# The opening of the Mamba stage: another order of transposes, softplus sums, copies, convolution and norm

## The chip, the cores and the metric

The kernel runs on one core of one Trainium2 chip. The metric is device time in microseconds (us) of one execution; the time before is 3008.5, the median of three runs (3007.97 to 3010.53). The engines are TensorE (PE, with its weight loads PEld), VectorE (DVE), ScalarE (ACT), GpSimd (POOL) and SyncE (SP, which issues DMAs). Each takes its own instructions in order and waits for the others by semaphores.

## The reference, cut to what matters

Four layers act on x of shape (2, 128, 56, 56), each as `x = x + layer(group_norm(x))`. Layer 0 is an attention, layer 1 a 3x3 convolution, layer 2 a mixture of experts on patches. Layer 3, in which the change lies, runs two Mamba blocks over the rows of the image, one from left to right and one from right to left, and fuses their outputs:

```python
xz = x @ in_w.T
xi, z = jnp.split(xz, 2, axis=-1)
xc = silu(conv_b + sum(xp[:, k:k + L, :] * conv_w[:, k] for k in range(K)))   # K = 4
dt, Bm, Cm = jnp.split(xc @ xproj_w.T, [DT_RANK, DT_RANK + D_STATE], axis=-1)
dt = softplus(dt @ dt_w.T + dt_b)
def step(h, inp):
    dA = jnp.exp(dt_l[:, :, None] * A)
    h = dA * h + (dt_l * u_l)[:, :, None] * B_l[:, None, :]
    return (h, jnp.einsum('bds,bs->bd', h, C_l))
y = (ys + xc * Dp) * silu(z)
return y @ out_w.T
```

The group norm in front of the layer needs the mean and the variance of a whole image, after the experts' results have been added to it.

## The kernel before, in words

The image is cut into 14 blocks of 448 positions (7 for each of the two images). In `mamba_pair` each block has two halves, forward (f) and backward (b), and each half 16 units: 8 pairs of states by 2 halves of the inner channels. For a unit, ScalarE computes `dA` (`decay`, two activations into PSUM), GpSimd `dBu` (`push`, the product of dtu and B, six buffers), VectorE scans (`scan`, L1939), and the state is multiplied by C, on VectorE from a PSUM copy `c_ps` (L1950, ScalarE writes the copy at L1927), or on GpSimd for the units listed in POOLED (L1948). TensorE sums the products into the PSUM tile `y` (`collect`, L1961; its first call also writes the skip term, L1957).

The order on every engine is written out by hand, in two stretches with a manual schedule. The first is the opening: steps below zero of an `agenda`, in which the first block's forward half is prepared. Its stages are the convolution (`conv`, into the banks "mm" and "c", 16 weight passes for both halves of the channels), `low`, `step`, `log`, `softplus` (a sum of four terms in PSUM by matmuls with the identity, L1874, and a copy of dt by ScalarE, L1875), `weigh` (dtu = dt * xc on VectorE, and a small memset of row starts on GpSimd) and `send_steps`: eight DMAs for each half of the channels, four that spread dtu (issued on SP) and four that spread dt (issued on GpSimd's queue). The second stretch is the loop over units; it also works off later agenda steps, each stage a few units ahead of its use: one TensorE operation, and its ScalarE copy one step later.

Among the opening's steps stands `arrive`, a generator for the second image: GpSimd gathers the experts' rows (g, 14 indirect DMAs), VectorE adds each pair of rows (L1486), TensorE transposes them (`y_ps`, L1489, four small transposes a block, seven blocks), VectorE adds them to x (L1462) and takes statistics (L88). After the seventh block follows the norm of the image (`norm_stages`: aggregate, two matmuls with a group matrix, and small VectorE and ScalarE operations, L66 to L110, and L1616 and L1617). A tuple of counts says how many pieces of this generator are worked off at each opening step. `back_bank` gives its PSUM from the "dA" banks while `opening` is true.

The first block's backward half has its convolution (`b.conv`) at opening steps 17, its Silu at step 19 (with a table load before and after), so that on the engines these stand among the first scans. The norm is first used by ScalarE when block 7 is prepared, some 190 units later.

Of the kernel before, what the change touches and what calls it, by code (L numbers as in the profile page):

```python
# [8 lines left out]
F32 = mybir.dt.float32  # L9
# [8 lines left out]
P = 128  # L18
# [1586 lines left out]
def arrive(net, combine, b, gathered, bank, banks, pool, norms, lead=0):  # L1605
    nc = net.nc
    yield from combine(b, gathered, bank, lead)
    got = []
    for n, stage in enumerate(net.norm_stages(b, banks, "mm", got.append)):
        fetch = stage()  # L1610
        if fetch:
            fetch()
        yield
    mean, rstd = got[0]
    both_of = pool.tile([P, 2], F32, name=f"norm{b}")
    nc.vector.scalar_tensor_tensor(both_of[:, 0:1], mean, -1.0, rstd, ALU.mult, ALU.mult)  # L1616
    nc.vector.tensor_copy(both_of[:, 1:2], rstd)  # L1617
    norms[b] = (both_of[:, 1:2], both_of[:, 0:1])


def mamba_pair(net, out, wts, combine, keep, norms):
# [19 lines left out]
    with ExitStack() as ctx:  # L1641
# [14 lines left out]

        def wide_bank(name):
            return ps.tile([P, 1024], F32, name=name, tag="dA", bufs=2)

        opening = True  # L1660

        def back_bank(name):
            return wide_bank(name) if opening else mm(name)

        class Banks:
            def tile(self, shape, dtype, name, tag):
                return back_bank(name)[:, :512]

        ps_of_norms = Banks()


        place = {"tag": "mm"}

        def mm(name):
            return ps.tile([P, 512], F32, name=name, tag=place["tag"])
# [93 lines left out]
        class Half:  # L1769
# [3 lines left out]
                self.blk, self.w = blk, w  # L1773
                self.dA, self.dBu, self.hc, self.C = {}, {}, {}, {}

            def conv(self, m, as_=AF.Identity):
                w = self.w
                pm = mm("conv_ps")
                for n in range(K):

                    at = n if w.d == "f" else 2 * (K - 1) - n
                    nc.tensor.matmul(
                        rows(pm[:, :BLK]),
                        w.conv[:, m, n, :],
                        self.blk.xn[:, :, at : at + HW],
                        start=n == 0,
                        stop=n == K - 1,
                    )
                if m == 0:
                    self.xc = work.tile([P, 2, BLK], F32, name="xc", tag=f"xc{w.d}", bufs=1 if w.d == "f" else 2)  # L1790
                return lambda: nc.scalar.activation(self.xc[:, m, :], pm[:, :BLK], as_, bias=w.conv_b[:, m : m + 1])
# [85 lines left out]
            def weigh(self, m=None):  # L1877

                some = slice(0, 2) if m is None else slice(m, m + 1)
                self.dtu = self.u  # L1880
                engine = nc.gpsimd if m is None else nc.vector
                engine.tensor_mul(self.dtu[:, some], self.dt[:, some], self.xc[:, some])

                at = 0 if self.w.d == "f" else HW - 1
                starts = self.dt[:, some].rearrange("p m (r t) -> p (m r) t", t=HW)[:, :, at : at + 1]
                nc.gpsimd.memset(starts, 1e31)

            def send_steps(self, m=None):

                some = slice(0, 2) if m is None else slice(m, m + 1)  # L1890
                if not m:
                    self.dt2 = work.tile([P, 2, 2, BLK], F32, name="dt2", tag="dt2")
                    self.dtu2 = work.tile([P, 2, 2, BLK], F32, name="dtu2", tag="dtu2")
                for to, src, queue in ((self.dtu2, self.dtu, nc.sync), (self.dt2, self.dt, nc.sync if m is None else nc.gpsimd)):
                    for s in range(2):
                        for r in range(2):
                            queue.dma_start(to[s * H : (s + 1) * H, some, r, :], src[r * H : (r + 1) * H, some, :])
# [87 lines left out]
        for n, blk in enumerate(blocks):  # L1985
# [3 lines left out]
            if n == 0:  # L1989
# [14 lines left out]
                    book(at + 12 + m, lambda f=f, m=m: f.send_steps(m))  # L2004
                for i, (h, m) in enumerate(((f, 0), (f, 1), (b, 0), (b, 1))):
                    book((1, 4, 5, 13)[i], lambda h=h, m=m: h.gate(m))
                book(at + 17, lambda b=b: b.conv(0))
                book(at + 17, lambda b=b: b.conv(1), tag="c")
                book(at + 19, lambda b=b: silu(b, None))
                for m in range(2):  # L2010
                    book(2 + 3 * m, lambda b=b, m=m: b.step(m))
                    book(4 + 3 * m, lambda b=b, m=m: b.log(m))
# [62 lines left out]

        E = mybir.EngineType
        with tc.manual_schedule(engines={E.PE, E.Activation, E.DVE, E.Pool, E.SP}):
            second = arrive(net, combine, 1, gathered, back_bank, ps_of_norms, keep, norms, LEAD2)
            first = min(agenda)
            for step in range(first, 0):  # L2080
                run(step)
                for _ in range((LEAD2, 0, 0, 0, 0, 0, 1, 0, 1, 2, 1, 1, 1, 2, 1, 1, 1)[step - first] if step - first < 17 else 0):
                    next(second, None)
                fetch(step + 1)
            opening = False
        with tc.manual_schedule(engines={E.PE, E.Activation, E.DVE, E.Pool, E.SP}):
            for h, u in units[:6:2]:
                h.send_c(u // 2)
# [3 lines left out]
            for n, (h, u) in enumerate(units):  # L2092
# [13 lines left out]
                if done:  # L2106
                    done.pop().close()
                waiting.append((h, u))

                quota = 0 if u == 3 and n > 3 else 2 if u == 7 and n > 7 else 1  # L2110
                for _ in range(quota):
# [124 lines left out]
```

## Time and profile before

| | |
|---|---|
| median of three runs | 3008.5 us |
| the profiled execution | 3005.48 us |
| its span on the core | 3003.3 us |
| TensorE, VectorE, ScalarE, GpSimd busy | 2679.8, 2187.2, 1851.7, 1450.4 us |
| the scans, L1939 | 448, 2.008 us each |
| dBu, L1920 | 448, 2.094 us each |
| first forward convolution of the Mamba stage | 1651.34 us |
| first scan | 1689.70 us |
| scan of unit 16 (first of the backward half) | 1752.98 us |
| last instruction's chain begins | 2962.88 us |

Times in the profile are microseconds from the span's start. In a row of a timeline the first number is the start, the second the length, then engine, line, operation, output and inputs, the number of instructions merged, and in brackets how long the engine had been idle and what ended that. A releaser is inferred; where the named engine had long been done, it was another. A table by stage gives for each stretch the busy time of each engine, the granted TensorE clock (1.00 is full), the share of DMA engines busy and GB/s.

### The profile page before, as it was taken

The numbers are of one execution on the slowest core, as the hardware profiler recorded it, in microseconds if no ns is written. First come the engines' busy times: TensorE is split into PE (matmuls) and PEld (weight loads), VectorE is DVE, ScalarE is ACT, GpSimd is POOL, SyncE is SP. The second block draws the span as 40 slices with busy tenths as digits, with TensorE's granted clock in tenths as the row PEclk, the third lists the DMA queues.
The fourth block names the chain that finished last, engine by engine and source line by source line (L and its number), as shares of the span: only waits on it lengthen the run. The fifth ranks groups of instructions, "written<-read, shape, count | busy, mean of one in ns | idle before, by whom it ended". The sixth has DMA issues, their size and how long they took to land. (4 is left out here: it accounts for less than half of the span.)

```text
span 3003.3 us, 39370 instructions
## 1 busy us (share of the span) xinstructions
PE 2679.8 (89%) x14926; PEld 1271.0 (42%) x14926; DVE 2187.2 (73%) x1856; ACT 1851.7 (62%) x2942; POOL 1450.4 (48%) x801
## 2 busy tenths in 40 slices
PE   7999999999989799999999788888888888888874
PEld 3333333333325688878777333333333333233321
DVE  5978999999886400000120589999999999999996
ACT  5778787888761100000011588888888888988884
POOL 3000010001322100000110789999999999999995
PEclk9999999999999799999999789999899999999997
DMA  1000000000002587878885644465554465544460
GB/s 56 1 1 1 1 1 1 1 1 1 1 1 61 224 316 295 330 295 329 312 300 211 146 112 115 121 142 140 118 121 118 115 145 131 127 116 121 116 149 23
DMA packets 157966, 369.30 MB, mean 123 GB/s; under 512 B 25190, under 2 KB 115014, under 8 KB 154166
## 3 DMA queue, kind: packets, MB, share of 16 engines
q1 hardware_dynamic: 135778, 339.30, 37.5%
q0 software_dynamic: 5520, 15.62, 1.7%
q10 hardware_dynamic: 16452, 11.61, 1.2%
q8 instruction: 122, 2.00, 0.3%
q14 instruction: 94, 0.77, 0.1%
HBM read 297.89 MB, written 17.20 MB: 105 GB/s over the span
## 5 line engine op out<-in xcount | busy, mean ns | idle before, releaser
L1920 POOL TENSOR_TENSOR dBu<-dtu,Bs 128x896 f32<-128x896 f32 x448 | 921.8, 2094 | 13.2 <-DVE h L1939 8.3
L1939 DVE TENSOR_TENSOR_SCAN h<-dA,dBu 128x896 f32<-128x896 f32 x448 | 881.7, 2008 | 25.9 <-ACT dA L1909 19.1
L620 ACT ACTIVATE ex<-sc 128x896 f32<-128x896 f32 (+1 forms) x700 | 602.6, 918 | 124.7 <-PE sc L617 113.4
L1961 PE MATMUL y<-h,both 128*64 128x448 f32 x1792 | 466.0, 611 | 81.8 <-POOL h L1948 74.3
L627 DVE TENSOR_TENSOR ex_sum<-ex_sum,ex 128x1792 f32<-128x1792 f32 (+1 forms) x238 | 492.6, 2070 | 35.2 <-ACT ex L620 21.2
L1380 PEld LDWEIGHTS h_ps<-xs_c,w 128*128 128x128 f32 x3584 | 406.6, 193 | 27.2 <-ACT ot L1403 16.2
L1380 PE MATMUL h_ps<-xs_c,w 128*128 128x128 f32 x3584 | 411.6, 277 | 6.9 <-DMA w<-in_L_conv_w_dram 5.3
L617 PE MATMUL sc<-q,k 32*128 32x448 f32 (+1 forms) x2800 | 403.6, 587 | 3.6 <-ACT ex L620 2.9
L1950 DVE TENSOR_TENSOR h<-h,c_ps 128x1792 f32<-128x1792 f32 (+1 forms) x168 | 326.6, 1944 | 26.7 <-ACT c_ps L1927 9.2
L635 PE MATMUL av<-ex,va 128*32 128x448 f32 (+1 forms) x2800 | 334.3, 552 | 0.1
L1394 DVE TENSOR_TENSOR ht<-h_ps,sg 128x512 f32<-128x512 f32 x56 | 38.5, 691 | 398.1 <-PE h_ps L1380 324.0
L582 POOL TENSOR_TENSOR a_e<-a_e,a_inv 112x784 f32<-112x784 f32 x14 | 41.6, 2973 | 583.3 <-ACT ex L620 394.5
L1909 ACT ACTIVATE dA<-dt,f_A 128x448 f32<-128x448 f32 x448 | 282.7, 636 | 58.4 <-DVE h L1939 45.5
L1909 ACT ACTIVATE dA<-dt,b_A 128x448 f32<-128x448 f32 x448 | 282.8, 635 | 34.9 <-DVE h L1939 25.5
L1961 PEld LDWEIGHTS y<-h,both 128*64 128x64 f32 x1792 | 118.3, 147 | 354.8 <-issue 209.0
L1314 POOL DMA_INDIRECT xr<-xd,whom x28 | 28.0, 1000 | 484.4 <-PE xr_ps L1369 444.5
L1948 POOL TENSOR_TENSOR h<-h,Cs 128x1792 f32<-128x1792 f32 (+1 forms) x70 | 252.6, 3609 | 12.6 <-PE sp_ps L1874 7.0
L617 PEld LDWEIGHTS sc<-q,k 32*128 32x128 f32 (+1 forms) x2800 | 137.7, 181 | 230.0 <-issue 132.3
L1392 ACT ACTIVATE sg<-h_ps 128x512 f32<-128x512 f32 x56 | 33.4, 597 | 306.2 <-PE h_ps L1380 306.2
L1400 PE MATMUL o_ps<-w,ht 128*128 128x512 f32 x448 | 201.2, 593 | 1.2 <-DVE ht L1394 1.2
L1403 ACT ACTIVATE ot<-o_ps,share 128x512 f32<-128x512 f32 x28 | 19.2, 687 | 246.5 <-PE o_ps L1400 246.5
L625 DVE TENSOR_TENSOR ex_sum<-ex 128x1792 f32<-128x1792 f32 x56 | 114.4, 2043 | 54.5 <-ACT ex L620 54.4
(346 smaller groups left out, 2983.3 us busy)
## 6 DMA issues: line engine op xcount, KB each, us to landing
w<-in_L_conv_w_dram SPq DMA_DIRECT2D x28, 4096.0 KB
w<-in_L_conv_w_dram SPq DMA_DIRECT2D x28, 2048.0 KB
Cs<-far SPq DMA_DIRECT2D x448, 112.0 KB
Bs<-far SPq DMA_DIRECT2D x54, 896.0 KB
dtu<-sp_u SPq DMA_DIRECT2D x108, 224.0 KB
dt<-dt SPq DMA_DIRECT2D x108, 224.0 KB
os<-ot ACTq DMA_DIRECT2D x28, 256.0 KB
xd<-xt SPq DMA_DIRECT2D x14, 224.0 KB
```

The lines of the kernel that those rows point to most:

```text
L617: nc.tensor.matmul(sc[:size, j, :BLK], self.m.k[rows, at : at + size], self.q[rows, :], start=True, stop=True)
L620: nc.scalar.activation(ex[:size, 2 * g : 2 * g + 2, :], sc[:size, :, :BLK], AF.Exp, scale=scale)
L627: nc.vector.tensor_add(self.total[g][:size], self.total[g][:size], ex[:size])
L635: nc.tensor.matmul(self.av[rows, :BLK], self.m.va[:size, i, rows], self.ex[i][:size, h, :], start=i == 0, stop=i == STEPS - 1,)
L1380: mm = nc.tensor.matmul(h_ps[:, i * SLOTS : (i + 1) * SLOTS], w1[:, q, f0 : f0 + P], xc[:, q, :], start=q == 0, stop=q == 3,)
L1400: mm = nc.tensor.matmul(o_ps, ht[:, i, :], w2[:, i, :], start=i == 0, stop=i == nj - 1)
L1909: nc.scalar.activation(self.dA[u][:, r * BLK : (r + 1) * BLK], self.dt2[:, m, r, :], AF.Exp, scale=self.w.A[:, j, 2 * m + r : 2 * m + r + 1],)
L1920: nc.gpsimd.tensor_tensor(self.dBu[u], self.dtu2[:, m], self.B[:, j, :].unsqueeze(1).to_broadcast(shape), ALU.mult)
L1939: nc.vector.tensor_tensor_scan(hf, af, bf, 0.0, ALU.mult, ALU.add)
L1948: nc.gpsimd.tensor_tensor(h4, h4, self.C[j].unsqueeze(1).to_broadcast(shape), ALU.mult)
L1950: nc.vector.tensor_tensor(h4, h4, self.c_ps[:, :BLK].unsqueeze(1).to_broadcast(shape), ALU.mult)
L1961: nc.tensor.matmul(self.y[r * H : (r + 1) * H, m, :BLK], both, self.hc[j][:, m, r, :], start=False, stop=j == PAIRS - 1)
```

## The change

It has four parts, all in the opening of `mamba_pair`.

1. The generator's pieces are dealt out in another way: on TensorE the third transpose comes after the first softplus sum, the fourth after the second sum, and the last three after that. Two came before both sums, and others between and after.
2. dt's copies (`send_steps` for one half of the channels) are issued on ScalarE's queue in place of GpSimd's; the memset of row starts in `weigh` goes to VectorE.
3. The first block's backward convolution moves ahead, to opening steps 10 and 13 (Silu at 15), and is written into the two banks of the PSUM tile `y`, which is not in use yet. On TensorE its first half stands ahead of the first softplus sum, its second half after the fourth transpose.
4. The second image's norm is no longer computed by small VectorE operations in the opening. `arrive_by_scalar` computes it in two pieces within the loop over units, after units 9 and 13: one aggregate on VectorE, two small matmuls in the bank "mm", and eleven small activations on ScalarE.

On TensorE the queue reads, before: low, transpose 1, dt 0 and 1, transposes 2, 3, 4, sum 0, transpose 5, sum 1, transposes 6, 7, two norm matmuls, both halves of the backward convolution, low of b. In the changed kernel: low, transpose 1, dt 0 and 1, transpose 2, first half of the backward convolution, sum 0, transpose 3, sum 1, transpose 4, second half of the convolution, transposes 5, 6, 7, low of b.

The diff, with unchanged lines left out:

```diff
+def arrive_by_scalar(net, combine, b, gathered, bank, later, pool, norms, lead):
+    nc = net.nc
+    yield from combine(b, gathered, bank, lead)
...
+    nc.gpsimd.memset(more, 1.5)
+    nc.vector.bn_aggr(mv, net.stats[b].rearrange("p k s -> p (k s)"))
+    ps = later("gn_ps")
+    nc.tensor.matmul(ps[:, 0:1], net.group, mv[:, 0:1], start=True, stop=True)
+    act(less, ps[:, 0:1], AF.Copy, scale=-1.0)
+    act(q, mv[:, 0:1], AF.Square, bias=less)
+    act(q, q, AF.Identity, bias=mv[:, 1:2])
+    yield
+    ps = later("gn_ps2")
+    nc.tensor.matmul(ps[:, 0:1], net.group, q, start=True, stop=True)
+    act(v, ps[:, 0:1], AF.Identity, bias=net.eps)
+    act(t, v, AF.Ln)
+    act(r, t, AF.Exp, scale=-0.5)
+    act(t, v, AF.Copy, scale=r)
+    act(t, t, AF.Copy, scale=r)
+    act(t, t, AF.Identity, scale=-0.5, bias=more)
+    act(both_of[:, 1:2], t, AF.Copy, scale=r)
+    act(both_of[:, 0:1], less, AF.Copy, scale=both_of[:, 1:2])
...
-            def conv(self, m, as_=AF.Identity):
+            def conv(self, m, as_=AF.Identity, ahead=False):
-                pm = mm("conv_ps")
+                if ahead and m == 0:
+                    self.room = ps.tile([P, 2, 512], F32, name="y", tag="y")
+                pm = self.room[:, m] if ahead else mm("conv_ps")
...
-                nc.gpsimd.memset(starts, 1e31)
+                (nc.gpsimd if m is None else nc.vector).memset(starts, 1e31)
...
-                for to, src, queue in ((self.dtu2, self.dtu, nc.sync), (self.dt2, self.dt, nc.sync if m is None else nc.gpsimd)):
+                for to, src, queue in ((self.dtu2, self.dtu, nc.sync), (self.dt2, self.dt, nc.sync if m is None else nc.scalar)):
...
-                book(at + 17, lambda b=b: b.conv(0))
-                book(at + 17, lambda b=b: b.conv(1), tag="c")
-                book(at + 19, lambda b=b: silu(b, None))
+                book(at + 10, lambda b=b: b.conv(0, ahead=True))
+                book(at + 13, lambda b=b: b.conv(1, ahead=True))
+                book(at + 15, lambda b=b: silu(b, None))
...
-            second = arrive(net, combine, 1, gathered, back_bank, ps_of_norms, keep, norms, LEAD2)
+            second = arrive_by_scalar(net, combine, 1, gathered, wide_bank, mm, keep, norms, LEAD2)
...
-                for _ in range((LEAD2, 0, 0, 0, 0, 0, 1, 0, 1, 2, 1, 1, 1, 2, 1, 1, 1)[step - first] if step - first < 17 else 0):
+                for _ in range((LEAD2, 0, 0, 0, 0, 0, 1, 0, 1, 0, 1, 1, 3, 1)[step - first] if step - first < 14 else 0):
...
+                if n in (9, 13):
+                    place["tag"] = "mm"
+                    next(second)
```

## The prediction

> **What bounds the kernel now.** I read the page's slices first (VectorE and GpSimd are at 9 tenths from slice 25 on, TensorE's clock is full nearly everywhere), then the stages by window, then each engine's timeline from 1640 to 1760 us. The stage table has, for each stretch, the stretch's length and busy time of TensorE, its weight loads, VectorE, ScalarE and GpSimd, then clock, DMA share and GB/s.
>
> ```profile
> 1645.00:1691.00 46.00, 32.19 (x89) 16.20 (x89) 17.85 (x50) 14.78 (x26) 20.48 (x25) 0.82 0.61 155
> 1691.00:1753.00 62.00, 48.42 (x120) 16.89 (x118) 46.84 (x28) 42.34 (x69) 48.40 (x23) 0.83 0.48 106
> 1753.00:1791.00 38.00, 35.99 (x104) 12.79 (x104) 34.61 (x20) 32.30 (x54) 35.35 (x18) 0.87 0.44 108
> 1791.00:2951.00 1160.00, 970.65 (x3292) 367.02 (x3291) 1125.76 (x642) 986.18 (x1768) 1137.25 (x538) 0.93 0.52 125
> ```
>
> From 1791 on VectorE is 97% and GpSimd 98% busy, and each waits for the other through six dBu buffers: no edit in the opening changes that stretch, it can only begin earlier. The whole change acts between 1651 and 1753, and its worth is how much earlier the scan of unit 16 (the backward half's first) comes than its 1752.98. GpSimd, by time (start, length, instruction, idle before and releaser):
>
> ```profile
> 1685.57 2.08 POOL L1920 TENSOR_TENSOR dBu<-dtu,Bs 128x896 f32<-128x896 f32 x1
> 1691.11 10.21 POOL L1920 TENSOR_TENSOR dBu<-dtu,Bs 128x896 f32<-128x896 f32 x5 [3.45 <-DMA dtu<-sp_u]
> ...
> 1707.23 2.08 POOL L1948 TENSOR_TENSOR h<-h,Cs 128x896 f32<-128x896 f32 x1
> 1709.27 14.34 POOL L1920 TENSOR_TENSOR dBu<-dtu,Bs 128x896 f32<-128x896 f32 x7
> 1730.64 3.98 POOL L1948 TENSOR_TENSOR h<-h,Cs 128x1792 f32<-128x1792 f32 x1 [7.04 <-PE sp_ps L1874]
> ...
> 1747.35 12.29 POOL L1920 TENSOR_TENSOR dBu<-dtu,Bs 128x896 f32<-128x896 f32 x6 [6.39 <-DVE h L1939]
> ```
>
> GpSimd's chain of multiplies starts for good at 1691.11, when the second group of dtu copies lands, and runs 18.2 us without a gap to 1709.31, the end of unit 2's h. The 7.04 us before 1730.64 are VectorE being late: that multiply needs scan 9, which ends at 1730.4. ScalarE shows why, and why the copies land late:
>
> ```profile
> 1678.27 0.53 ACT L1875 COPY dt<-sp_ps 128x448 f32<-128x448 f32 x1 [1.90 <-PE sp_ps L1874]
> 1681.74 0.53 ACT L1875 COPY dt<-sp_ps 128x448 f32<-128x448 f32 x1 [2.94 <-PE sp_ps L1874]
> ...
> 1716.22 0.53 ACT L1804 COPY zs<-gate_ps 128x448 f32<-128x448 f32 x1
> 1720.12 0.53 ACT L1875 COPY dt<-sp_ps 128x448 f32<-128x448 f32 x1 [3.36 <-PE sp_ps L1874]
> 1721.75 0.63 ACT L1850 ACTIVATE sp_e<-dt_ps,c_L_conv_b_dt_b 128x448 f32<-128x448 f32 x1 [1.10 <-PE dt_ps L1839]
> ...
> 1723.89 0.52 ACT L1927 COPY c_ps<-Cs 128x448 f32<-128x448 f32 x1
> ```
>
> The last row releases VectorE at 1724.44 after 4.48 us idle (the multiply of units 6 and 7); scan 8 follows at 1726.38. Two rows each of TensorE and VectorE complete the picture: the softplus sums stand behind the fourth transpose, which waits for a returned row, and run at half clock; and small VectorE operations last 1.6 to 2.0 us.
>
> ```profile
> 1671.78 0.99 PE L1489 MATMUL y_ps<-ident,g 112*128 112x112 f32 x4 [4.50 <-issue]
> 1672.56 1.73 PE L1874 MATMUL sp_ps<-sp_e,ident 128*128 128x448 f32 x2
> ```
>
> ```profile
> 1691.64 1.55 DVE L69 TENSOR_TENSOR ir_t<-ir_v,gn_rstd 128x1 f32<-128x1 f32 x1
> 1693.23 2.00 DVE L70 SCALAR_TENSOR_TENSOR ir_t<-ir_t,gn_rstd 128x1 f32<-128x1 f32 x1
> ```
>
> **Part 1: the order of TensorE's work.** The inputs of the first sum are ready when its sp_w ends, 1666.09. In the changed kernel the queue holds transpose 2, the backward convolution's first half, sum 0, transpose 3, sum 1. Transpose 2 ends at 1664.42 as before. The convolution's 8 passes cost 3.2 us at full clock (16 in 6.35 at 1651.34) and about 6.0 at half (0.745 a pass, 1688.51 on). The clock was halved at 1663.95. When does it come back? By the rows, the sums began at 1672.56 and the clock was full from 1677.7, 5.1 us later. The Trainium skill (TensorE: Matmul & The Clock Gate, "Part 1: The HAM clock gate") has about 3.4 us of sustained work. By the row 6.8 passes are slow and the convolution ends at 1669.9; by the rule 4.6 are, and it ends at 1669.1. I take the row; 0.8 us is this term's bound. Sum 0 at full clock (3.2 us, 1678.52 to 1681.70) gives its dt copy at 1673.3, 5.0 earlier. Transpose 3 (0.62) and sum 1 give the second copy at 1677.2, 4.5 earlier. The later transposes (7 in both kernels) come among work that no longer waits for them; the sums of x on VectorE end near 1685.6 to 1687 (1686.30 now), which only the first scan waits for.
>
> **Part 2: the copies.** After each dt copy VectorE weighs (0.63) and now sets the 128x8 starts itself: GpSimd took 0.11, VectorE's smallest rows 0.14 to 0.16, so 0.15 each, in front of one add of returned rows. dtu's four copies follow on SP, dt's four on ScalarE. An issue costs 0.33 on ScalarE (its os copy) to 0.6 on SP, so 2.6 to 4.8 us of ScalarE for eight; GpSimd is rid of 4.2 us (1680.06 to 1685.56). What stands behind them on ScalarE is the second dt copy and the second conv Identity; both have 1 us to spare. Here a rule speaks against the edit: DMA: Bandwidth & Descriptors ("Issuing engines are not separate DMA queues") says that all queues end on the same 16 engines and another queue saves issue time only. The row agrees on the point: GpSimd issued until 1685.56 and multiplied at 1685.57, but then waited for dtu, which was SP's, till 1691.11, with the DMA share at 1.0. A gain of the 4.2 us would be wrong; by rule and row the queue itself gives 0. What counts is when dtu's second group starts: 1682.96 now, 1678.5 after. It took 8.15 us to land; the same gives 1686.6, 4.5 earlier. Bounds: 1685.0 (the copies of B come behind it) to 1688.5 (sixteen copies now share eight completion counters between the two queues, so each of the second group waits until one of the first has landed, and 2.4 us of returned rows are still in flight).
>
> **Part 3: what leaves the unit loop.** Both conv Identities (0.63 each), two table loads (1.28 each), Silu (0.95), one convolution (6.2 at half clock) and the norm's stretched VectorE operations (1.55, 2.00, 0.18, 2.00, 0.14 = 5.9) no longer stand among scans 0 to 3; with them goes the 4.02 us idle before 1705.31. They don't bring 10 us: GpSimd paces these scans. Its 18.2 us from 1686.6 end at 1704.8. Then TensorE reads unit 2's h and the chain to c_ps follows: now 1714.24 to 1724.44, 10.2 us at full clock, of which the sum is 3.3. TensorE reached it 4.9 us after GpSimd had finished, because low, gate, dt and skip ran late and at half clock (0.57 over 1700 to 1710); afterwards it waits there for GpSimd. But a TensorE that waits is slow: with gate (1.86 instead of 1.04), sum (5.7, the 1672.56 sum) and their neighbours at half clock the chain is 14.2. Between these ends I take 12.0, a clock that returns during the sum, as in the 1710 to 1720 stretch (0.92): units 6 and 7's multiply at 1716.8, 7.6 earlier (5.4 to 10).
>
> **Part 4: the norm on ScalarE.** It comes back inside the loop, three activations at unit 9 and eight at unit 13, each 0.20 by the 128x1 rows plus 0.04 between dependent ones. At unit 9 ScalarE waits for scan 9, the aggregate (0.34 on VectorE), a matmul (0.35) and two handovers (0.6 each): dA of unit 11 is 1.9 late against a scan of slack, and VectorE loses 1.6, of which 1.5 reaches the next c_ps. At unit 13 the eight (2.0 us) stand between dA 14 and dA 15, straight after Silu and two table loads (4.4), where VectorE waits already (1.24 at 1745.16). Behind them are dA 15, zs, low (3.3 from zs to its copy, 1746.75 to 1750.05) and c_ps, for which VectorE waits 1.95 now. So scan 16 is later by 1.6 + 2.0 = 3.6. Bounds 2.0 (low at full clock: 1.6 less) and 5.0 (0.28 for an activation, the ln_t row, and a late matmul).
>
> **Sum.** 7.6 - 3.6 = 4.0 us. On the profiled execution, 3005.48 us with a span of 3003.3, that is 3001.5; its median lies 3.0 higher, so 3004.5.
>
> **Rivals.** *TensorE stays warm* (0.26): the chain takes 10.2, the copies land at 1685.5, and low is fast too: 10.5 - 2.5 = 8, 3000.5. For it: gate, y and gate follow one another from 1701. Against: mixed narrow matmuls at 1746.8 to 1759 stayed at half. *The lead is used up* (0.14): half clock throughout (5.4) against the norm's upper bound (5.0): 0.4, 3008. *The copies go one after the other* (0.12), the slower side: the shared counters hold the second group until the first has landed. The first starts at 1674; with 8.15 us and 2.4 behind returned rows it lands at 1684.5, the second, 8.15 later and with B's 3.3 among it, at 1695.9, 4.8 later than now. Then the chain to units 6 and 7 ends 0 to 4 late, plus 3.6 to 5: about 6.5 slower, 3015. It decides from a landing after 1690.6; before that, part 3 covers it. Against it: DMA moves over 215 GB/s there, and 0.9 MB need 4.3 us.
>
> **Chances.** The likeliest case has 0.48, its own range 3002 to 3008. About 6 us (0.2%) is what a measurement tells from no change: faster by more than that takes the warm case and 0.08 of the likeliest, 0.34; slower 0.12; within, 0.54. Leaving out the end of the warm case and nearly all of the serial one gives 2998.5 to 3012.
>
> **What would show it.** dt copies near 1673 and 1677; dBu's continuous run from 1686 to 1687; no VectorE operation of 2 us on 128x1 after it; TensorE's clock at the first backward sum (the dearest unknown); a wait for dA 11 and for the c_ps after the eight activations; scan 16 at about 1749. It is wrong if the second group's landing does not move with its issue, if VectorE's wait for c_ps before units 6 and 7 goes away, or if the lead at scan 16 isn't kept to the end.

## The result and the profile after

The changed kernel takes 3003.3 us (median of twenty runs, 2997.5 to 3010.8); the kernel before, beside it, 3008.8 us (twenty runs, 3004.9 to 3015.6). The ratio is 0.9981, 95% interval 0.9974 to 0.9987. Of 3008.8 us that is 5.7 us less (3.9 to 7.8), at the edge of the 0.2% that was named as what a measurement can tell.

One thing has to be settled before any row is read. The profiled execution of the changed kernel took 3010.8 us (span 3009.1), which is the longest of its twenty, and its Mamba stage began late: the first forward convolution starts at 1657.33, where before had 1651.34. Nothing of the change stands ahead of that convolution. So all times are compared from it: in this profile, 5.99 us is taken off ("aligned") to stand beside a time of before. In the first row of the table by stage (length, busy time of TensorE, its weight loads, VectorE, ScalarE, GpSimd, then clock, DMA share, GB/s) the same bounds therefore cut other work than in the table of before, by 6 us:

```profile
1645.00:1691.00 46.00, 38.29 (x109) 18.74 (x107) 16.71 (x48) 15.48 (x24) 16.79 (x15) 0.95 0.61 153
...
```

It holds the whole backward convolution, which before began only at 1688.51: TensorE is busy 38.3 us where it had been 32.2, at a clock of 0.95 (0.82). GpSimd, by time (start, length, line, operation, shapes, count, and in brackets the idle time before it with what ended it):

```profile
1687.64 2.34 POOL L1940 TENSOR_TENSOR dBu<-dtu,Bs 128x896 f32<-128x896 f32 x1 [6.56 <-DMA Cs<-far]
1692.87 10.36 POOL L1940 TENSOR_TENSOR dBu<-dtu,Bs 128x896 f32<-128x896 f32 x5 [2.90 <-DMA dtu<-sp_u]
...
1709.17 2.08 POOL L1968 TENSOR_TENSOR h<-h,Cs 128x896 f32<-128x896 f32 x1
1711.21 14.31 POOL L1940 TENSOR_TENSOR dBu<-dtu,Bs 128x896 f32<-128x896 f32 x7
1727.70 3.97 POOL L1968 TENSOR_TENSOR h<-h,Cs 128x1792 f32<-128x1792 f32 x1 [2.19 <-issue]
```

GpSimd's continuous run starts at 1692.87, aligned 1686.88, and unit 2's h ends at 1711.25, aligned 1705.26: the forecast had 1686.6 and 1704.8. The 7.04 us that GpSimd had waited for a late VectorE are 2.19. On TensorE these are the first half of the convolution, the first sum and, further on, the reading of unit 2's h:

```profile
1670.20 4.51 PE L1802 MATMUL y<-pad,b_conv_t 128*128 128x448 f32 x8
1674.55 0.91 PE L1894 MATMUL sp_ps<-sp_e,ident 128*128 128x448 f32 x2
...
1711.30 0.97 PE L1981 MATMUL y<-h,both 128*64 128x448 f32 x4 [1.40 <-POOL h L1968]
```

ScalarE, in the opening and then up to the copy that releases units 6 and 7 (ACTq is its queue of issues):

```profile
1677.75 0.53 ACT L1895 COPY dt<-sp_ps 128x448 f32<-128x448 f32 x1 [0.96 <-PE sp_ps L1894]
1679.16 2.87 ACTq L1917 DMA_DIRECT2D dt<-dt  x4
1682.07 0.53 ACT L1895 COPY dt<-sp_ps 128x448 f32<-128x448 f32 x1 [3.79 <-PE y_ps L1489]
1685.10 3.98 ACTq L1917 DMA_DIRECT2D dt<-dt  x4
1689.12 0.63 ACT L1811 ACTIVATE xc<-y,c_L_conv_b_conv_b 128x448 f32<-128x448 f32 x1 [6.51 <-PE y_ps L1489]
...
1717.17 0.53 ACT L1895 COPY dt<-sp_ps 128x448 f32<-128x448 f32 x1 [3.36 <-PE sp_ps L1894]
1718.81 0.63 ACT L1870 ACTIVATE sp_e<-dt_ps,c_L_conv_b_dt_b 128x448 f32<-128x448 f32 x1 [1.11 <-PE dt_ps L1859]
...
1720.95 0.52 ACT L1947 COPY c_ps<-Cs 128x448 f32<-128x448 f32 x1
```

The dt copies stand at aligned 1671.76 and 1676.08 (forecast 1673.3 and 1677.2). TensorE now waits 1.40 us for unit 2's h, where it had come 4.9 us after its end. The chain from there to the c_ps copy keeps its two idle pieces (3.36 and 1.11 against 3.36 and 1.10). VectorE's rows that answer to those of before: its multiply of units 6 and 7, a scan behind the norm's first piece, one behind the eight activations, and the multiply ahead of scan 16:

```profile
1721.50 2.02 DVE L1970 TENSOR_TENSOR h<-h,c_ps 128x1792 f32<-128x1792 f32 x1 [6.15 <-ACT c_ps L1947]
...
1732.28 2.02 DVE L1959 TENSOR_TENSOR_SCAN h<-dA,dBu 128x896 f32<-128x896 f32 x1 [2.59 <-ACT dA L1929]
...
1748.32 2.02 DVE L1959 TENSOR_TENSOR_SCAN h<-dA,dBu 128x896 f32<-128x896 f32 x1 [1.53 <-ACT dA L1929]
1752.96 2.02 DVE L1970 TENSOR_TENSOR h<-h,c_ps 128x1792 f32<-128x1792 f32 x1 [2.62 <-ACT c_ps L1947]
```

The wait for c_ps ahead of units 6 and 7 did not go; it grew from 4.48 to 6.15 us, since the scans before it come sooner. The multiply stands at aligned 1715.51, 8.9 us earlier than before. Then waits for dA (2.59 and 1.53 us) and a longer one for c_ps (2.62 where it had been 1.95) give half of it back; some 1.6 us of the 2.59 belong to the clock and not to the norm, as before_again and norm_spread will show. Scan 16 starts at 1754.90, aligned 1748.91. The forecast was "about 1749".

The following table holds all profiles of this study, in us from the first forward convolution, and the timed ratio of each against the kernel before. "Loop" is the stretch from scan 40 to scan 447, "half" the time in it during which the granted TensorE clock was 0.5, the only value beside 1.0 that the profiles have.

| kernel | second dt copy | dBu run | h of unit 2 ends | units 6, 7 | scan 8 | scan 12 | scan 16 | scan 40 | loop | half | ratio (95%) |
|---|---|---|---|---|---|---|---|---|---|---|---|
| before | 30.40 | 39.77 | 57.97 | 73.10 | 75.04 | 86.52 | 101.64 | 171.59 | 1150.1 | 175.9 | 1 |
| before, again | 29.98 | 39.34 | 57.55 | 72.68 | 74.62 | 87.80 | 102.91 | 172.82 | 1148.5 | 183.2 | |
| after | 24.74 | 35.54 | 53.91 | 64.16 | 66.11 | 80.14 | 97.57 | 166.36 | 1156.7 | 201.4 | .9981 (.9974, .9987) |
| after, again | 26.41 | 36.51 | 55.40 | 65.66 | 67.61 | 81.80 | 99.27 | 166.95 | 1151.6 | 187.7 | .9978 (.9968, .9988) |
| undo_order | 29.54 | 37.78 | 56.02 | 67.03 | 68.97 | 83.16 | 100.58 | 168.23 | 1154.7 | 201.3 | .9985 (.9974, .9997) |
| dt_on_pool | 23.94 | 32.76 | 53.28 | 63.90 | 65.85 | 80.03 | 97.32 | 164.82 | 1157.3 | 214.3 | .9990 (.9982, .9998) |
| conv_back | 24.46 | 36.74 | 54.98 | 66.16 | 68.10 | 82.29 | 99.72 | 168.23 | 1154.8 | 208.2 | .9984 (.9977, .9990) |
| norm_opening | 26.65 | 35.38 | 56.35 | 68.50 | 70.45 | 81.94 | 97.02 | 164.60 | 1151.7 | 187.7 | .9979 (.9971, .9986) |
| norm_alone | 30.46 | 39.91 | 58.13 | 69.21 | 71.15 | 83.64 | 100.98 | 168.51 | 1155.0 | 198.0 | .9991 (.9983, .9999) |
| norm_spread | 24.83 | 34.98 | 53.93 | 64.31 | 66.26 | 79.33 | 94.44 | 164.48 | 1152.1 | 184.3 | .9979 (.9972, .9985) |
| spread_pool_split | 25.85 | 34.85 | 53.23 | 63.48 | 65.42 | 78.60 | 93.72 | 161.36 | 1156.7 | 199.8 | .9966 (.9953, .9979) |

Three things have to be kept in mind with this table. The two profiles of the changed kernel differ by 1.7 us at scan 16, so a difference of one or two microseconds between two single profiles is not yet an effect of an edit. From scan 16 to scan 40 the length goes with the clock: 67.5 to 68.5 us where 3.4 to 6.8 us of the stretch are at half clock (after again, undo_order, dt_on_pool, conv_back, norm_opening, norm_alone, spread_pool_split), 68.8 with 10.1 (after), and about 70 with 13.7 to 16.9 (both of before, norm_spread). Scan 16 therefore compares the kernels better than scan 40. And in all eleven profiles the clock stays at one value for 3.41 us or a multiple of it: its changes lie on a grid, and this grid lies differently against the first convolution in every profile.

### The profile page after: what moved, and what is told of

Its sections match the earlier page's. It is cut to its first block, busy times and chain, and to the rows that moved or that the text cites. A ratio compares the mean times of both kernels' runs of the same rounds, so it can differ in the third digit from the quotient of the medians.

```text
span 3009.1 us, 39362 instructions
## 1 busy us (share of the span) xinstructions
PE 2688.4 (89%) x14926; PEld 1273.6 (42%) x14926; DVE 2180.9 (72%) x1849; ACT 1854.5 (62%) x2951; POOL 1446.6 (48%) x792
## 5 line engine op out<-in xcount | busy, mean ns | idle before, releaser
L1400 PE MATMUL o_ps<-w,ht 128*128 128x512 f32 x448 | 201.3, 593 | 1.2 <-DVE ht L1394 1.2
## 6 DMA issues: line engine op xcount, KB each, us to landing
w<-in_L_conv_w_dram SPq DMA_DIRECT2D x28, 2048.0 KB, 10.3
```

Of the source, the lines that this page charges most:

```text
L1400: mm = nc.tensor.matmul(o_ps, ht[:, i, :], w2[:, i, :], start=i == 0, stop=i == nj - 1)
```

## The experiments

The first question was which part brings the lead. My theory was the forecast's: dtu's copies land earlier (parts 1 and 2), GpSimd's chain paces the first scans, part 3 clears the way for it, and the norm takes half back later. The rival put the gain into the norm's leaving the opening, and a third theory into the queue.

**undo_order**: part 1 undone, the tuple of counts deals the transposes out as before.

```diff
-for _ in range((LEAD2, 0, 0, 0, 0, 0, 1, 0, 1, 0, 1, 1, 3, 1)[step - first] if step - first < 14 else 0):
+for _ in range((LEAD2, 0, 0, 0, 0, 0, 1, 0, 1, 2, 1, 1, 1, 1)[step - first] if step - first < 14 else 0):
```

> The changed kernel with the third and fourth transposes dealt out ahead of the first softplus sum again; the rest as changed. Theory (the lead comes from the second group of dtu copies landing earlier, and GpSimd's chain from there): the sums wait for the fourth returned row again, the first dt copy comes about 20.5 us after the stage's first forward convolution begins in place of 20.4 - the convolution sits in front, so TensorE is warm: about 24 us; GpSimd's continuous dBu run starts 3 to 4 us later than in the changed kernel, 39 us after that convolution; of the 5.5 us gain 1.5 to 2.5 stay. Rival (the lead comes from taking the convolution, Silu and table loads out of the first scans): the order costs under 1 us, 4.5 to 5.5 stay.

Measured: 3004.9 us, ratio 0.9985 (0.9974 to 0.9997). The first softplus sum waits for a returned row again:

```profile
1664.27 4.63 PE L1802 MATMUL y<-pad,b_conv_t 128*128 128x448 f32 x8
...
1672.39 0.71 PE L1489 MATMUL y_ps<-ident,g 112*128 112x112 f32 x4 [3.03 <-DVE g L1486]
1672.93 0.93 PE L1894 MATMUL sp_ps<-sp_e,ident 128*128 128x448 f32 x2
```

The sums stand behind that idle time of 3.03 us again: the second dt copy is at 29.54 from the convolution (24.74 and 26.41 in the two profiles of the changed kernel), GpSimd's run 1.3 to 2.2 us later, units 6 and 7 1.4 to 2.9 later, scan 16 1.3 to 3.0 and scan 40 1.3 to 1.9 later. So part 1 is worth between 1 and 3 us in the opening. My theory had asked for more (GpSimd's run 3 to 4 us later), and the timed ratios do not tell the part from nothing.

**dt_on_pool**: dt's copies back on GpSimd's queue.

```diff
-(self.dt2, self.dt, nc.sync if m is None else nc.scalar)
+(self.dt2, self.dt, nc.sync if m is None else nc.gpsimd)
```

> The changed kernel with dt's copies back on GpSimd's queue; the rest as changed (the small memset stays on VectorE). Theory from the trace (SP and ScalarE share completion counters, so the second group's first dtu copy was issued 2.0 us after its memset and ScalarE was held to 31.8 us after the first convolution): SP issues without that wait, dBu's continuous run starts 1 to 2 us earlier (33.5 to 34.5 us after the first convolution, 35.5 in the changed kernel), the first scan 3 us earlier, total 1 to 2 us faster than the changed kernel. The prediction's view (the queue gives nothing): equal within 1. Rival (GpSimd's time was the point): 2 to 4 us slower than the changed kernel.

Measured: 3006.4 us, ratio 0.9990 (0.9982 to 0.9998). What SP's queue waited for (us in total, times, longest), in the changed kernel from 1676 to 1692:

```profile
SPq L1917 <- DVE dt L1906: 5.4, 1, 5.4
SPq L1853 <- DMA dt<-dt: 1.8, 1, 1.8
SPq L1845 <- DMA dtu<-sp_u: 1.1, 1, 1.1
...
```

And the whole answer for dt_on_pool, from 1670 to 1684:

```profile
SPq L1917 <- DVE dt L1906: 6.0, 2, 5.6
```

With dt on ScalarE, SP waits for transfers of dt before it may issue a copy of C that does not read dt; with dt on GpSimd it waits for no transfer. That is the wait that the forecast's upper bound had named, and the semaphores in the trace confirm its reason: the copies of SP and of ScalarE signal their landing on the same eight semaphores in turn, those of GpSimd on eight others. The second copy of C was issued at 1684.67, 0.02 us after the dt copy that had used its semaphore had landed. The issues of four copies on ScalarE took 2.87 and 3.98 us, such waits included. GpSimd in dt_on_pool:

```profile
1684.27 6.15 POOL L1940 TENSOR_TENSOR dBu<-dtu,Bs 128x896 f32<-128x896 f32 x3 [1.14 <-DMA dtu<-sp_u]
1692.65 4.11 POOL L1940 TENSOR_TENSOR dBu<-dtu,Bs 128x896 f32<-128x896 f32 x2 [2.23 <-DVE h L1959]
1696.72 3.98 POOL L1968 TENSOR_TENSOR h<-h,Cs 128x1792 f32<-128x1792 f32 x1
```

Its run begins 2.8 us earlier than in the first profile of the changed kernel (0.8 of it because the second dt copy stands earlier), but stops after three, for 2.23 us. So only 0.6 us is left at the end of unit 2's h. The multiply of unit 4 is the first that reads the second load of B. The releaser named is a scan, but what ended the wait was B: the last copy of its second load was issued 28.36 us after the first convolution and landed at 41.02, and the multiply starts at 41.14. In the first profile of the changed kernel this copy was issued 4.7 us later and landed only 0.6 us later, at 41.62. Where that load is waited for, norm_opening's trace names it:

```profile
1695.31 4.10 POOL L1945 TENSOR_TENSOR dBu<-dtu,Bs 128x896 f32<-128x896 f32 x2 [0.38 <-DMA Bs<-far]
```

The queue is thus worth nothing or a little less than nothing in the opening (without it scan 16 is 0.3 to 2.0 us earlier), while the timed ratios lean the other way by 2.7 us, with intervals that overlap. My theory's gain of 1 to 2 us in time did not come; the part's size, and even its sign, stays open.

**conv_back**: part 3 undone, the backward convolution back at step 17 in its old banks, the Silu at 19.

```diff
-                book(at + 10, lambda b=b: b.conv(0, ahead=True))
-                book(at + 13, lambda b=b: b.conv(1, ahead=True))
-                book(at + 15, lambda b=b: silu(b, None))
+                book(at + 17, lambda b=b: b.conv(0))
+                book(at + 17, lambda b=b: b.conv(1), tag="c")
+                book(at + 19, lambda b=b: silu(b, None))
```

> The changed kernel with the first block's backward convolution and its Silu back at opening steps 17 and 19, in the banks mm and c; the rest as changed. Theory (GpSimd paces the first scans): scans 2 and 3 come 4 to 8 us later again, but the multiply of units 6 and 7 only 0 to 2.5 us later, by low and gate of the backward half coming late; 3 to 5.5 of the 5.5 us gain stay. Rival (the convolution between the scans was the cost): nearly all of the gain goes, 0 to 1.5 us stay.

Measured: 3004.0 us, ratio 0.9984 (0.9977 to 0.9990). Scan 3 comes at 48.20 instead of 43.17, 5.0 us later (2.6 against the second profile of the changed kernel); yet unit 2's h ends only 1.1 later (0.4 earlier), units 6 and 7 2.0 (0.5) and scan 16 2.2 (0.5). GpSimd's rows show why the five microseconds do not pass through: it multiplies without a gap.

```profile
1688.12 10.22 POOL L1940 TENSOR_TENSOR dBu<-dtu,Bs 128x896 f32<-128x896 f32 x5 [3.99 <-DMA dtu<-sp_u]
1698.29 3.99 POOL L1968 TENSOR_TENSOR h<-h,Cs 128x1792 f32<-128x1792 f32 x1
1702.25 2.08 POOL L1940 TENSOR_TENSOR dBu<-dtu,Bs 128x896 f32<-128x896 f32 x1
```

This is the forecast's sentence "GpSimd paces these scans", confirmed for the convolution, and the theory of this run held.

**norm_spread**: the same aggregate, matmuls and eleven activations, but booked one or two at a time at agenda steps 71 to 108, many units after unit 13.

```diff
-            second = arrive_by_scalar(net, combine, 1, gathered, wide_bank, mm, keep, norms, LEAD2)
+            second = combine(1, gathered, wide_bank, LEAD2)
-                if n in (9, 13):
-                    place["tag"] = "mm"
-                    next(second)
+        for s, piece in norm_pieces(net, 1, mm, keep, norms):
+            book(s, piece)
...
+    return (71, aggregate), (72, means), (104, deviations), (106, root), (107, newton), (108, end)
```

> The changed kernel with the norm's pieces cut smaller and booked at units 71 to 109, each activation a step after its matmul, in places where the bank mm is free; the rest as changed. Theory (the norm at units 9 and 13 costs 4.9 us of the lead, 8.93 at scan 8 to 4.08 at scan 16): scan 16 comes 8 to 9 us earlier than before relative to the first forward convolution, and the whole is 3 to 5 us faster than the changed kernel, some 9 us faster than before. Rival (what is lost there is the ordinary wait for the PSUM copy of C and for low, whatever stands in front): at most 1 us. Second rival (the saturated stretch takes any lead back, as in the profiled run, where 5.2 us at scan 40 had become -1.4 at scan 447): scan 16 is earlier, the total is not.

Measured: 3001.4 us, ratio 0.9979 (0.9972 to 0.9985). From scan 8 to scan 16 it takes 28.2 us; the changed kernel took 31.5 and 31.7. Those 3.3 to 3.5 us are the price of the norm at units 9 and 13: about 1.0 at unit 9 (VectorE's wait for dA is 2.59 us in the changed kernel and still 1.55 here) and 2.3 between scans 12 and 16. At scan 16 its lead over before is 7.2 us, 3.1 to 4.8 more than the changed kernel's. A total 3 to 5 us below the changed kernel had been expected; the timed ratios do not separate the two.

The second question was whether the norm's leaving the opening brings anything by itself.

**norm_opening**: part 4 undone, the rest kept (`arrive` with its norm in place of `arrive_by_scalar`, three more counts for its pieces, no pieces at units 9 and 13; a small class that gives the norm's matmuls their bank is left out).

```diff
-            second = arrive_by_scalar(net, combine, 1, gathered, wide_bank, mm, keep, norms, LEAD2)
+            second = arrive(net, combine, 1, gathered, wide_bank, ps_of_norms, keep, norms, LEAD2)
-(LEAD2, 0, 0, 0, 0, 0, 1, 0, 1, 0, 1, 1, 3, 1)[step - first] if step - first < 14 else 0
+(LEAD2, 0, 0, 0, 0, 0, 1, 0, 1, 0, 1, 1, 3, 1, 1, 1, 2)[step - first] if step - first < 17 else 0
-                if n in (9, 13):
-                    place["tag"] = "mm"
-                    next(second)
```

> The changed kernel with the norm computed in the opening again, by the small VectorE and ScalarE operations of before, after the seventh transpose; the other three parts as changed. Theory (GpSimd paces the first scans and hides the norm there; at units 9 and 13 nothing hides it): the small VectorE operations of 2 us come back among the first scans, but scan 8 comes 7.5 to 9 us earlier than before relative to the first forward convolution, as in the changed kernel (8.9), scan 16 as much, and scan 40 is 6 to 8 us earlier (5.2 in the changed kernel); total 1 to 3 us faster than the changed kernel. Rival (VectorE's 5.9 us there were a cost): scan 8 only 3 to 4 us earlier, total no faster than the changed kernel or slower.

Measured: 3003.9 us, ratio 0.9979 (0.9971 to 0.9986), the same as the changed kernel. VectorE's first scan waits behind the norm's chain:

```profile
1692.19 0.16 DVE L107 COPY gn_mean<-gn_ps 128x1 f32<-128x1 f32 x1 [2.38 <-PE gn_ps L104]
...
1692.96 1.99 DVE L110 SCALAR_TENSOR_TENSOR gn_q<-gn_d,gn_mv 128x1 f32<-128x1 f32 x1
1695.69 0.16 DVE L66 TENSOR_SCALAR ir_v<-gn_ps 128x1 f32<-128x1 f32 x1 [0.74 <-PE gn_ps L116]
1696.72 2.02 DVE L1964 TENSOR_TENSOR_SCAN h<-dA,dBu 128x896 f32<-128x896 f32 x1 [0.87 <-ACT dA L1934]
```

GpSimd then waits for the late scans before its first multiply by C:

```profile
1701.71 3.97 POOL L1973 TENSOR_TENSOR h<-h,Cs 128x1792 f32<-128x1792 f32 x1 [2.30 <-DVE gn_rstd L71]
```

So unit 2's h ends at 56.35 although the run of dBu began as early as in the changed kernel, and scan 8 comes at 70.45, 2.8 to 4.3 us later than there. My theory had scan 8 7.5 to 9 us ahead of before; it is 4.6 ahead, which is nearer to the rival: in this order VectorE's norm is not hidden behind GpSimd. But nothing is paid at units 9 and 13, and scan 16 comes at 97.02, where the changed kernel has 97.57 and 99.27. The norm has two places here, and the timed ratios give them the same price.

**norm_alone**: the kernel before with part 4 only.

```diff
...
-second = arrive(net, combine, 1, gathered, back_bank, ps_of_norms, keep, norms, LEAD2)
+second = arrive_by_scalar(net, combine, 1, gathered, back_bank, mm, keep, norms, LEAD2)
-(LEAD2, 0, 0, 0, 0, 0, 1, 0, 1, 2, 1, 1, 1, 2, 1, 1, 1)[step - first] if step - first < 17 else 0
+(LEAD2, 0, 0, 0, 0, 0, 1, 0, 1, 2, 1, 1, 1, 1)[step - first] if step - first < 14 else 0
+                if n in (9, 13):
+                    place["tag"] = "mm"
+                    next(second)
```

> The kernel before with the norm at units 9 and 13 on ScalarE alone (part 4), nothing else changed. Theory: the opening gains nothing that lasts, since GpSimd's chain starts as before, 39 to 40 us after the first forward convolution; scan 8 within 1.5 us of before; the norm costs 3.5 to 5 us between scans 8 and 16; scan 40 3 to 5 us later than before, total 2 to 5 us slower. Rival (VectorE's small operations were the cost): scan 8 4 to 6 us earlier, total about equal.

Measured: 3006.5 us, ratio 0.9991 (0.9983 to 0.9999): a little faster, where my theory had it slower. GpSimd's run and the end of unit 2's h stay where they were (39.91 and 58.13 against 39.77 and 57.97), and still units 6 and 7 come 3.9 us earlier. TensorE tells why. First the kernel before, then norm_alone:

```profile
1686.83 0.35 PE L104 MATMUL gn_ps<-gn_mv,group 128*128 128x1 f32 x2 [2.44 <-DVE gn_mv L100]
1688.09 0.56 PE L116 MATMUL gn_ps<-gn_q,group 128*128 128x1 f32 x2 [0.91 <-DVE gn_q L110]
1688.51 9.32 PE L1782 MATMUL conv_ps<-pad,b_conv_t 128*128 128x448 f32 x16
...
1714.24 0.97 PE L1961 MATMUL y<-h,both 128*64 128x448 f32 x4
```

```profile
1689.87 6.26 PE L1812 MATMUL conv_ps<-pad,b_conv_t 128*128 128x448 f32 x16
...
1715.94 0.97 PE L1991 MATMUL y<-h,both 128*64 128x448 f32 x4
```

Before, two norm matmuls stood in TensorE's queue ahead of the backward convolution. TensorE idled 2.44 and 0.91 us for them, and the convolution behind them ran partly at half clock: 0.58 us a pass, against 0.39 in norm_alone. Everything of the backward half (xc, low, gate, dt, skip) came late, and TensorE reached unit 2's h 4.9 us after GpSimd had finished it (1714.24 less 1709.31). In norm_alone it is there 0.9 us after (the h ends at 1715.06). So the 3.9 us came through TensorE's queue, in which the two matmuls waited for VectorE's aggregate and gn_q. VectorE's long small operations among the scans did not hold GpSimd up here: its run did not move. How much of the 3.9 is the idle time and how much the slow convolution, this run does not separate. Of this, 3.2 us are lost again by scan 16 (1.5 if the second profile of before, below, is taken), and at scan 16 it leads by 0.7 (1.9).

**spread_pool_split**: norm_spread, dt on GpSimd's queue as in dt_on_pool, and the second load of B cut in two.

```diff
-                book(at + 14, lambda f=f: f.send_b(slice(2, PAIRS)))
+                book(at + 14, lambda f=f: f.send_b(slice(2, 4)))
+                book(at + 14, lambda f=f: f.send_b(slice(4, PAIRS)))
```

> The changed kernel with the norm spread over units 71 to 109, dt's copies on GpSimd's queue, and the second load of B cut in two (pairs 2 and 3 first). Theory (with dt on GpSimd's queue the second group lands 2.8 us earlier, but GpSimd then stood 2.2 us at unit 4 for pairs 2 to 7 of B): the wait at unit 4 goes, unit 2's multiply ends 50.5 to 51.5 us after the first forward convolution (53.9 in the changed kernel, 53.3 with the queue alone), scan 16 comes 9 to 10.5 us earlier than before and scan 40 9 to 10; total about 9 us faster than before. Rival (the DMA bytes are the bound, in whatever order): the wait moves to unit 6, scan 40 as with the spread norm alone, 7 us. Second rival (TensorE at half clock takes the place of GpSimd): multiply of units 6 and 7 no earlier than 63 us after the convolution.

Measured: 3000.6 us, ratio 0.9966 (0.9953 to 0.9979), the fastest of all: 10.2 us below the kernel before. Five multiplies stand in a row now:

```profile
1686.42 10.35 POOL L1988 TENSOR_TENSOR dBu<-dtu,Bs 128x896 f32<-128x896 f32 x5 [1.32 <-DMA dtu<-sp_u]
```

But the cut of B's load brought nothing that shows. The run begins 2.1 us later than in dt_on_pool (the second dt copy comes 1.9 us later), the multiply of unit 4 starts at 41.0 as it did there, and unit 2's h ends at 53.23 (53.28 there), where 50.5 to 51.5 had been expected. The lead over before is 7.9 us at scan 16, 0.7 more than norm_spread's; that it is 10.2 at scan 40 (7.1) goes with the clock behind scan 16. The kernel is surely faster than before, on five runs; its interval still touches that of the changed kernel, and its lead over norm_spread is not shown.

The third question came from the profiles themselves: at the last scan the first profile of the changed kernel is 1.4 us *later* than that of before. Is the lead lost in the loop?

**after_again**: the changed kernel, unchanged.

> The changed kernel once more, for the spread of one and the same program. Theory (the stretch from scan 40 to scan 447 varies with the time that TensorE spends at half clock in it, 1150 us at 176 us of half clock to 1157 at 214 in the six profiles so far): scans 0 to 40 as in its first profile within 0.5 us, the stretch anywhere from 1150 to 1158 us, and on the line through those six. Rival (the change itself made the stretch 6.6 us longer): 1156 to 1158 again.

**before_again**: the kernel before, unchanged.

> The kernel before, unchanged, for a second profile of it. If the loop's length in a profiled execution is set by how the granted clock falls and not by the kernel, the stretch from scan 40 to scan 447 will again not be that of the first profile (1150.1 us at 175.9 us of half clock) but anything within 1148 to 1158 us, longer where the half-clock time is longer; the opening's scans will stand within 2 us of the first profile's, counted from the first forward convolution (scan 16 at 101.6, scan 40 at 171.6). If the changed kernel made the loop itself slower, the stretch stays near 1150 us.

Measured: after_again 3003.8 us, ratio 0.9978 (0.9968 to 0.9988); before_again one run, 3006.6 beside 3007.2. Scan 16 of after_again stands 1.7 us later than in the first profile, where 0.5 had been allowed for. The same program has a loop of 1156.7 us in one profile and 1151.6 in another. Over the eleven profiles the loop goes with its time at half clock: 1148.5 to 1152.1 where that is 176 to 188 us, 1154.7 to 1157.3 where it is 198 to 214. Both profiles of before are short ones, so on the profiles alone one could not exclude that the changed kernels' loop is a microsecond or two longer. The timed runs bound that: over the two profiles of each kernel the mean lead is 3.9 us at scan 16 and 5.6 at scan 40, and the timed gain is 5.7 (3.9 to 7.8). The lead of the opening is kept.

The second profile of before also shows the clock in the opening. Its second backward sum, behind the same 3.12 us of idle time, ran at half clock for part of the way; in the first profile it did not (0.92 us for each of the last three pairs). Behind the rows stand three steps of the grid with the clock of each, 1.00, 0.50 and 1.00 (columns as in the table by stage):

```profile
1728.12 1.02 PE L1874 MATMUL sp_ps<-sp_e,ident 128*128 128x448 f32 x2 [3.12 <-ACT sp_w L1863]
1728.98 1.44 PE L1874 MATMUL sp_ps<-sp_w,minus 128*128 128x448 f32 x2
1730.21 1.70 PE L1874 MATMUL sp_ps<-sp_u,ident 128*128 128x448 f32 x2
1731.71 1.38 PE L1874 MATMUL sp_ps<-dt,ident 128*128 128x448 f32 x2
...
1725.82:1729.23 3.41, 1.11 (x3) 0.68 (x4) 3.41 (x2) 3.35 (x7) 0.00 (x0) 1.00 0.19 67
1729.23:1732.65 3.42, 3.42 (x6) 1.33 (x4) 3.33 (x3) 1.31 (x3) 1.12 (x1) 0.50 0.00 0
1732.65:1736.06 3.41, 3.41 (x12) 1.38 (x11) 1.75 (x2) 1.71 (x3) 3.41 (x2) 1.00 0.00 0
```

One step at half clock makes the stretch from scan 8 to scan 12 1.7 us longer (13.18 in place of 11.48), and scan 16 comes later with it.

**Which part brings the lead?** Undone one at a time, no part changes the timed ratio beyond the overlap of the intervals, and at scan 16 none takes away more than 3.0 us. The parts overlap. TensorE reads unit 2's h 4.9 us after its end in the kernel before, but 0.9 after it with part 4 alone (norm_alone), 1.0 with part 4 but not part 3 (conv_back), 1.9 with part 3 but not part 4 (norm_opening), and 0.1 with both. Either of the two removes most of the lateness.

## Why the prediction was right

The forecast was 3004.5 us, 4.0 below before, from 7.6 at units 6 and 7 less 3.6 for the norm. Measured were 5.7 us (3.9 to 7.8), and, between the first profiles, 8.9 at units 6 and 7 and 4.1 at scan 16; between the second ones 7.0 and 3.6. The mechanism was right. Of the 7.6, the copies were to give 4.5 and gave 4.1 and 2.2; the chain behind them was to give 3.1 and gave 4.9 in both. That the sum came out is in part luck: the two errors have opposite signs, and the clock alone moves single terms by 1 to 2 us.

- *Part 1, right.* The forecast weighed the row's 5.1 us for the return of the clock (the convolution's first half ends at 1669.9) against the 3.4 of the Trainium skill (TensorE: Matmul & The Clock Gate, "Part 1: The HAM clock gate"; 1669.1). In the two profiles of the changed kernel it ended at aligned 1668.7 and 1670.4, and both estimates lie between. The clock returned 2.6 us after the convolution's start in the one and 4.5 us in the other, each time at a point of the 3.41 us grid. So 3.4 us is the grid's step; no single delay from the start of the work, neither 3.4 nor 5.1, fits both. undo_order shows the order itself to be worth between 1 and 3 us.
- *Part 2, right in time, and its bounds too.* GpSimd's run began at aligned 1686.88 and 1687.85; forecast 1686.6, bounds 1685.0 to 1688.5. The sentence "the queue itself gives 0" is not contradicted: the wait between the two queues, put there as the upper bound's reason, is real, and without it the run begins up to 2.8 us earlier. What the forecast missed is that B's landing then stands next. It took the 18.2 us of GpSimd's run as free of gaps, and in the second profile of the changed kernel they were 18.9, with 0.61 us of waiting for B. The Trainium skill (DMA: Bandwidth & Descriptors, "Issuing engines are not separate DMA queues") says that all issuers' copies run on the same 16 engines; dt_on_pool agrees, where B's load was issued 4.7 us earlier and landed 0.6 earlier.
- *Part 3, right for the convolution, incomplete for the norm.* conv_back shows "GpSimd paces these scans". But in the kernel before, the norm's "stretched VectorE operations" were not the part of it that cost: its two matmuls in TensorE's queue were. (In norm_opening, where GpSimd's run begins earlier, VectorE's part costs too: the 2.30 us above.) The forecast had seen TensorE reach unit 2's h 4.9 us late "because low, gate, dt and skip ran late", and did not follow that back to the two idle times ahead of the convolution. norm_alone prices it at 3.9 us. The sum did not suffer, because each of parts 3 and 4 removes most of the same lateness.
- *The chain from unit 2's h to the multiply, mis-sized.* Between 10.2 (full clock) and 14.2 I took 12.0. From the end of unit 2's h it was 10.3 in both profiles of the changed kernel and 10.4 in norm_spread: gate 1.03, sum 0.92 a pair. "A TensorE that waits is slow" does not hold for its 1.40 us of waiting here, and does for 3.12 a little later. This term gave 1.8 us more than forecast in both.
- *Part 4, mis-sized in appearance.* From scan 8 to scan 16 the changed kernel lost 4.9 us on before, where the forecast had 3.6. Of that, the second backward sum at half clock makes up to 1.7: before_again, which has it as well, takes 28.3 us against 26.6. With like clocks the norm costs 3.2 to 3.5 (31.5 less 28.3, or 31.7 less norm_spread's 28.2), so 3.6 was right as a sum; of its two pieces unit 9 cost 1.0 (forecast 1.6) and unit 13 2.3 (2.0). At unit 13 the eight activations took 2.40 us, not 2.0:

```profile
1744.61 0.24 ACT L1639 ACTIVATE few<-gn_ps,eps 128x1 f32<-128x1 f32 x1
1744.89 0.20 ACT L1640 ACTIVATE few<-few 128x1 f32<-128x1 f32 x1
...
1745.36 0.29 ACT L1642 ACTIVATE few<-few 128x1 f32<-128x1 f32 x1
...
1746.72 0.29 ACT L1646 ACTIVATE norm<-few,norm 128x1 f32<-128x1 f32 x1
1746.93 1.29 ACT L1929 ACTIVATE dA<-dt,f_A 128x448 f32<-128x448 f32 x2
```

  The last five, each with a scale or a bias that an earlier one or a memset wrote, last 0.29 to 0.30, the first three 0.20 to 0.24. The stretch from scan 12 to scan 16 is 2.3 us longer than before's, and with the norm spread it is before's again (15.1 us).
- *The rivals.* "TensorE stays warm" was right about the chain, not about the total at scan 16. "The copies go one after the other" was half there: the waits between the queues show, the longest of them 1.8 and 2.0 us in the two profiles, and the landing stayed 2.7 to 3.7 us short of the point from which that rival decides.
- *Behind scan 16.* From there to scan 40, before took 70.0 and 69.9 us, the changed kernel 68.8 and 67.7. The forecast had nothing here. As told below the table, over the eleven profiles this goes with the half-clock time of the stretch and with no one part of the change (norm_opening takes 67.6, norm_alone 67.5, norm_spread 70.0). So the 1 to 2 us by which the profiles' lead grows here go with the clock. Whether the change brings that clock about, or it is chance, stays open.

## What to carry to other kernels

Follow a late engine back to its first idle time, not only to the slow rows in front of the wait: taking the norm with its two matmuls of 0.35 and 0.56 us out of TensorE's queue was worth 3.9 us at units 6 and 7, because TensorE had idled for them and a convolution behind them then ran slowly. Work that is moved out of a crowded stretch still has a price where it lands; at scan 16 it was cheapest spread one or two pieces at a time over later units (3.1 to 4.8 us more lead than in two lumps), though the timed runs do not confirm the difference. And a gain of 0.2% cannot be read from the end of two profiles: count from a common mark near the change, take a second profile of the same program, and let the timed runs decide.

## What was not expected of the hardware

- Two profiles of one program differ by 5 us in the loop (1156.7 and 1151.6), with 201 and 188 us of half clock in it. In all eleven, the clock changes only at multiples of 3.41 us.
- The same 3.12 us of idle time on TensorE was followed by full clock in one profile of before (0.92 a pair of passes) and by half clock in the other (1.44 and 1.70).
- With copies issued on SP and on ScalarE, SP's queue waited 1.8 us for ScalarE's transfers, which its own copy does not read but whose eight completion semaphores it shares; with the copies on GpSimd's queue it waited for none.
